# A two-layer selective-scan block: softplus from one Exp, carries and products two states at a time, old y added on VectorE

## The chip, the cores and the metric

One core of a Trainium2 chip runs the whole program. The metric is device time in microseconds (us) of one execution, the median of three runs. The engines are named as the profile names them: PE (TensorE, with PEld for its weight loads), DVE (VectorE), ACT (ScalarE), POOL (GpSimd) and SP, whose queue issues the DMAs.

## What is computed

Two layers of a vision state-space model work on x of shape (4, 64, 64, 192) in fp32. Only the first layer is touched. For each of 4 images it makes u (384 channels at 4096 positions) and a gate z by a projection, and then runs four selective scans: k = 0 along rows, k = 1 along columns, k = 2 and 3 the same two backwards. Cut to what matters:

```python
delta = jax.nn.softplus(delta + delta_bias[None, :, None])
def step(h, inp):
    dt, ut, bt, ct = inp
    dA = jnp.exp(dt[..., None] * A_k[None])
    dBu = dt[..., None] * bt[:, :, None, :] * ut[..., None]
    h = dA * h + dBu
    y = jnp.einsum('bkdn,bkn->bkd', h, ct)
    return (h, y)
# 16 states n, 384 channels d, 4096 steps, 4 directions k, 4 images
y = out_y[:, 0] + inv_y[:, 0] + wh_y + invwh_y     # the four directions are summed
```

A normalisation, the gate and an output projection follow. The second layer is of the same kind, written in another way.

## The kernel before

The method `scans` of `FirstLayer` runs once per image. An **item** is one direction k and one chunk of 512 positions: 4 x 8 = 32 items per image, first those of k = 0 and 2 alternating, then, from item 16, those of k = 1 and 3. Each item goes through 16 **states** n, so a step of the main loop is one state of one item, numbered g; an image has 512 of them. A tile of 128 partitions x 3 x 512 holds the 384 channels as three blocks d of 128.

One state of one item takes:

- ACT: `b_product` (L716), four scalings of dt*u by B, token by token, two states ahead; `decay` (L728), three Exps with a scale per partition, one state ahead.
- PE: `turn_x` (L733), three times four transposes of 128 x 128 that bring the product from tokens to channels in PSUM; the tile x has three buffers.
- DVE: `scan` (L741), three scans of 512 columns that read a from SBUF and x from PSUM and write h. After the third, a small tensor_reduce (L751) copies the last column of the three blocks into a tile `carry`, from which the next item of this direction starts.
- POOL: `c_product` (L755), h times C over 128 x 1536, in place. It can't begin before the reduce has read h.
- PE: `add_y` (L768), three times four transposes that add h into the item's y in PSUM (tiles yp), three states later. Because yp has one buffer, states 0 and 1 of an item are added in its state 4, and state 2, 3, ... in its state 5, 6, ...

The tile h has seven buffers of one state each. y of the four directions is summed in DRAM: `load("yold")` fetches what is there, `start_y` (L762) puts it into yp by a matmul with the identity in states 3 and 4, `end_y` (L781) copies yp out on DVE in states 2 and 3 of the next item, and a DMA stores it. yold is fetched in state 5 for the item after it, if that has the same kind of direction; otherwise, at item 16, only when the item before has been stored, in state 3.

All four engines run in an order written out by hand, and each engine takes its instructions in that order. In step g the order is: ACT's prepared steps, b_product(g+2), decay(g+1); then for each block d: scan(g, d) on DVE, turn_x(g+1, d) on PE, and the add_y steps that are due on PE; then PE's prepared steps, c_product(g) and POOL's prepared steps. The prepared steps make delta, B and dt*u of coming items. The method `steps` of `Item` lists each as (items ahead, state, engine, function); those of (2, 13) run in state 13 of the item two before. Softplus is computed as max(v, 0) + log(1 + e), with e = exp(-|v|):

- `dt_rows` (L632): v from a matmul of 13 rows into PSUM, in states 7 to 9 two items ahead and once more in states 5 to 7 one item ahead. The PSUM tiles dp, tp, bp and zp share two buffers.
- `absolute` (L638) and `exp` (L641) on ACT in states 10 to 12 and 13, into tile e, which has one buffer.
- `plus` (L645) and `minus` (L649) on POOL in states 14 and 15: 1 + e rounded, and what remains when 1 is taken away again; `log` (L652) on ACT, `rest` (L655) and `total` (L658) on POOL in states 2, 1 and 4 one item ahead. `rest` and `total` add what the rounding lost, so that small delta stay exact.
- `delta` (L661) on DVE in states 7 to 9, then `turn` (L675) and `times_u` (L681) in states 10 to 13.

The first eight items of an image also make the gate: one matmul step on PE and one copy on ACT in each of three states (`gate_in`, `gate_out`).

Of the kernel before, what the change touches and what calls it, by code (L numbers as in the profile page):

```python
# [10 lines left out]
F32 = mybir.dt.float32  # L11
# [8 lines left out]
LC = 512  # L20
# [382 lines left out]
class FirstLayer:  # L403
# [168 lines left out]
    def scans(self):  # L572
        nc, tc = self.tc.nc, self.tc
        with ExitStack() as ctx:
            pool = lambda name, bufs, **k: ctx.enter_context(tc.tile_pool(name=name, bufs=bufs, **k))
            p1, p2, p3, p7 = pool("b1", 1), pool("b2", 2), pool("b3", 3), pool("b7", 7)
# [4 lines left out]
            ident = self.ident  # L581
# [22 lines left out]
            class Item:  # L604
# [30 lines left out]
                def absolute(self, d):  # L635
                    if d == 0:
                        self.e = p1.tile([128, ND, LC], F32, name="e")
                    nc.scalar.activation(self.e[:, d, :], self.dp[d], AF.Abs)  # L638

                def exp(self):  # L640
                    nc.scalar.activation(self.e, self.e, AF.Exp, scale=-1.0)  # L641

                def plus(self):
                    self.wl = p1.tile([128, ND, LC], F32, name="wl")
                    nc.gpsimd.tensor_scalar(self.wl, self.e, 1.0, 1.0, ALU.add, ALU.mult)  # L645

                def minus(self):
                    self.dt = p2.tile([128, ND, LC], F32, name="dt")
                    nc.gpsimd.tensor_scalar(self.dt, self.wl, -1.0, 1.0, ALU.add, ALU.mult)  # L649

                def log(self):
                    nc.scalar.activation(self.wl, self.wl, AF.Ln)  # L652

                def rest(self):
                    nc.gpsimd.tensor_tensor(self.e, self.e, self.dt, ALU.subtract)  # L655

                def total(self):
                    nc.gpsimd.tensor_tensor(self.e, self.e, self.wl, ALU.add)  # L658

                def delta(self, d):  # L660
                    nc.vector.scalar_tensor_tensor(  # L661
                        self.dt[:, d, :], self.dp[d], 0.0, self.e[:, d, :], ALU.max, ALU.add
# [22 lines left out]
                def steps(self):  # L685
# [3 lines left out]
                    for d in range(ND):  # L689
                        r += [(2, 7 + d, "pe", s(self.dt_rows, d)), (2, 10 + d, "act", s(self.absolute, d))]  # L690
                    r += [(2, 13, "act", self.exp), (2, 14, "pool", self.plus), (2, 14, "pool", self.load_u)]
                    r += [(2, 15, "pool", self.minus), (1, 2, "act", self.log)]
# [17 lines left out]
            carry, xTs, xs, as_, hs, cs = {}, {}, {}, {}, {}, {}  # L710
# [26 lines left out]
            def scan(g, d):  # L737
                it, n = flat[g]
                if d == 0:
                    hs[g] = p7.tile([128, ND, LC], F32, name="h")  # L740
# [4 lines left out]
                    0.0 if it.first else carry[it.k, n][:, d : d + 1],  # L745
# [3 lines left out]
                if d == ND - 1:  # L749
                    kept = carry[it.k, n] = pk.tile([128, ND], F32, name=f"carry{it.k // 2}_{n}")  # L750
                    nc.vector.tensor_reduce(kept, last(hs[g], it.k), mybir.AxisListType.X, ALU.max)  # L751
# [5 lines left out]
            def start_y(it, b):  # L757

                if b == 0:
                    it.yp = [ps_y.tile([128, LC], F32, name=f"yp{i}") for i in range(ND)]  # L760
                yo = it.yold.rearrange("p j e -> p (j e)")[:, b * LC : (b + 1) * LC]
                nc.tensor.matmul(it.yp[b], ident, yo, start=True, stop=False, skip_group_check=True)  # L762

            def add_y(g, b):
                it, n = flat[g]
                for i in range(NJ):
# [5 lines left out]
                        start=False,  # L772
# [5 lines left out]
            def end_y(it, b):  # L778
                if b == 0:
                    it.yt = p1.tile([128, NJ, DI], F32, name="yt")  # L780
                nc.vector.tensor_copy(it.yt.rearrange("p j e -> p (j e)")[:, b * LC : (b + 1) * LC], it.yp[b])  # L781
# [16 lines left out]
            with tc.manual_schedule(engines={nc.tensor.engine, nc.scalar.engine, nc.vector.engine, nc.gpsimd.engine}):  # L798
# [18 lines left out]
                items[0].yold = load("yold", self.y_dram, items[0].k, items[0].c)  # L817
# [8 lines left out]
                for g in range(N + LAG + 1):  # L826
# [11 lines left out]
                    if it is not None:  # L838
                        for at, b in (((LAG, 1), 0), ((LAG, 2), 1), ((LAG + 1, 0), 2)):
# [793 lines left out]
```

## Time and profile before

| what | us |
|---|---|
| median of 3 runs | 11103.35 (11099.11 to 11105.88) |
| the profiled execution's own time | 11106.54 |
| its span, first to last instruction | 11104.6 |
| DVE busy | 9693.3 (87%) |
| ACT busy | 9775.8 (88%) |
| POOL busy | 8587.9 (77%) |
| PE busy | 9551.9 (86%) |
| one scan stage, first to last c_product of an image | 2192 to 2197, four times |

Some of the costliest groups of instructions of the first layer's scans (duration: mean of one):

| line, engine | what | count | ns |
|---|---|---|---|
| L755 POOL | h times C | 2048 | 3470 |
| L741 DVE | scan with a carry | 5376 | 1266 |
| L716 ACT | b_product | 8192 | 609 |
| L728 ACT | decay | 6144 | 716 |
| L751 DVE | carry | 2048 | 158 |
| L762 PE | old y into PSUM | 768 | 664 |
| L638, L641, L652 ACT | Abs; Exp; Log | 384; 128; 128 | 585; 1478; 1485 |
| L645, L649 POOL | plus; minus | 128; 128 | 1478; 1482 |
| L655, L658 POOL | rest; total | 128; 128 | 3460; 3477 |

Instructions of one engine overlap, so the distance from one start to the next is shorter than a duration. A wait is shown as idle time with the engine and line that ended it. PE's clock is granted at full or half rate, and the trace has a record of it.

### The profile page before, as it was taken

The numbers are of one execution on the slowest core, as the hardware profiler recorded it, in microseconds if no ns is written. First come the engines' busy times: TensorE is split into PE (matmuls) and PEld (weight loads), VectorE is DVE, ScalarE is ACT, GpSimd is POOL, SyncE is SP. The second block draws the span as 40 slices with busy tenths as digits, with TensorE's granted clock in tenths as the row PEclk, the third lists the DMA queues.
The fourth block names the chain that finished last, engine by engine and source line by source line (L and its number), as shares of the span: only waits on it lengthen the run. The fifth ranks groups of instructions, "written<-read, shape, count | busy, mean of one in ns | idle before, by whom it ended". The sixth has DMA issues, their size and how long they took to land. (4 is left out here: it accounts for less than half of the span.)

```text
span 11104.6 us, 172135 instructions
## 1 busy us (share of the span) xinstructions
PE 9551.9 (86%) x61449; PEld 7273.6 (66%) x61449; DVE 9693.3 (87%) x11515; ACT 9775.8 (88%) x16979; POOL 8587.9 (77%) x2776
## 2 busy tenths in 40 slices
PE   7998888888988888888988888889988888788677
PEld 4776666666776666656776666657766766655366
DVE  4999899976999899968999899949998999878675
ACT  5999999977999999969999999959999999856477
POOL 3999899955999899938999899929998999700370
PEclk8999999998999999998999999989999999989688
DMA  4333344344333344443333433353333434433458
GB/s 125 109 108 101 91 101 101 98 137 127 109 106 101 92 101 99 98 159 112 109 103 96 98 97 99 93 168 109 109 99 95 98 98 98 120 119 123 157 131 272
DMA packets 833671, 1267.54 MB, mean 114 GB/s; under 512 B 102026, under 2 KB 517655, under 8 KB 832292
## 3 DMA queue, kind: packets, MB, share of 16 engines
q1 hardware_dynamic: 827940, 1250.15, 40.5%
q0 software_dynamic: 4864, 6.29, 0.4%
q8 instruction: 488, 8.00, 0.3%
q14 instruction: 379, 3.10, 0.1%
HBM read 955.83 MB, written 300.42 MB: 113 GB/s over the span
## 5 line engine op out<-in xcount | busy, mean ns | idle before, releaser
L755 POOL TENSOR_TENSOR h<-h,bct 128x1536 f32<-128x1536 f32 x2048 | 7062.9, 3470 | 579.9 <-DVE carry L751 477.5
L741 DVE TENSOR_TENSOR_SCAN h<-a,carry,x 128x512 f32<-128x512 f32 x5376 | 6604.9, 1266 | 231.0 <-PE x L733 194.9
L733 PE MATMUL x<-ident,xT 128*128 128x128 f32 x24576 | 4000.8, 287 | 811.8 <-DVE h L741 710.1
L716 ACT ACTIVATE xT<-dtuT,bT 128x384 f32<-128x384 f32 x8192 | 4358.8, 609 | 93.0 <-PE x L733 87.3
L733 PEld LDWEIGHTS x<-ident,xT 128*128 128x128 f32 x24576 | 2804.0, 145 | 2136.5 <-DVE h L741 920.5
L728 ACT ACTIVATE a<-dt,A_log_f 128x512 f32<-128x512 f32 x6144 | 3977.7, 716 | 0.0
L768 PE MATMUL yp<-ident,h 128*128 128x128 f32 x24576 | 3703.1, 277 | 9.2 <-POOL h L755 9.2
L768 PEld LDWEIGHTS yp<-ident,h 128*128 128x128 f32 x24576 | 2944.2, 144 | 78.8 <-issue 62.6
L632 PE MATMUL dp<-xd,w_dtb_f 13*128 13x512 f32 x1536 | 882.7, 657 | 216.0 <-DVE dt L661 211.3
L741 DVE TENSOR_TENSOR_SCAN h<-a,x 128x512 f32<-128x512 f32 x768 | 899.1, 1207 | 191.3 <-PE x L733 114.0
L645 POOL TENSOR_SCALAR wl<-e 128x1536 f32<-128x1536 f32 x128 | 189.2, 1478 | 799.3 <-ACT e L641 406.2
L519 PE MATMUL pp<-xT,w_in 96*128 96x512 f32 x1152 | 539.2, 617 | 1.1 <-DVE xw L562 1.1
L632 PEld LDWEIGHTS dp<-xd,w_dtb_f 13*128 13x128 f32 x1536 | 235.0, 189 | 456.6 <-DVE dt L661 341.3
L762 PE MATMUL yp<-yold,ident 128*128 128x512 f32 x768 | 445.1, 664 | 72.7 <-DMA yold<-y 72.7
L1137 DVE SCALAR_TENSOR_TENSOR acc<-pad,conv_w_s,acc 128x2048 f32<-128x2048 f32 x192 | 439.3, 2342 | 53.5 <-ACT acc L1135 52.9
L638 ACT ACTIVATE e<-dp 128x512 f32<-128x512 f32 x384 | 224.7, 585 | 269.3 <-DVE dt L661 155.4
L1118 POOL MEMSET pad<- 128x66 f32 x12 | 1.9, 158 | 578.4 <-DVE acc L1137 458.9
L658 POOL TENSOR_TENSOR e<-e,wl 128x1536 f32<-128x1536 f32 x128 | 445.1, 3477 | 0.3
L655 POOL TENSOR_TENSOR e<-e,dt 128x1536 f32<-128x1536 f32 x128 | 442.9, 3460 | 0.3
L751 DVE TENSOR_REDUCE carry<-h 128x3 f32<-128x3 f32 x2048 | 322.7, 158 | 70.4
L519 PEld LDWEIGHTS pp<-xT,w_in 96*128 96x128 f32 x1152 | 221.3, 198 | 244.4 <-issue 234.3
L661 DVE SCALAR_TENSOR_TENSOR dt<-dp,e 128x512 f32<-128x512 f32 x384 | 255.5, 666 | 65.2 <-POOL e L658 58.7
(170 smaller groups left out, 6875.3 us busy)
## 6 DMA issues: line engine op xcount, KB each, us to landing
bct<-xp SPq DMA_DIRECT2D x1024, 512.0 KB, 4.9
uT<-uT SPq DMA_DIRECT2D x64, 768.0 KB, 4.7
yold<-y SPq DMA_DIRECT2D x64, 768.0 KB, 7.9
y<-yt SPq DMA_DIRECT2D x64, 768.0 KB, 4.5
uT<-uT SPq DMA_DIRECT2D x128, 384.0 KB, 5.0
yold<-y SPq DMA_DIRECT2D x128, 384.0 KB, 5.3
y<-yt SPq DMA_DIRECT2D x128, 384.0 KB, 4.6
zg<-gate SPq DMA_DIRECT2D x64, 768.0 KB, 6.3
```

The costliest lines, as they stand in the source:

```text
L519: self.tc.nc.tensor.matmul(pp, self.w_in[:, i, e * 128 : (e + 1) * 128], self.xT[:, i, t * LC : (t + 1) * LC], start=(i == 0), stop=(i == ...
L632: nc.tensor.matmul(self.dp[d], w, self.xd[0 : DR + 1, :], start=True, stop=True)
L655: nc.gpsimd.tensor_tensor(self.e, self.e, self.dt, ALU.subtract)
L658: nc.gpsimd.tensor_tensor(self.e, self.e, self.wl, ALU.add)
L716: nc.scalar.mul(xTs[g][:, j, :], it.dtuT[:, j * DI : (j + 1) * DI], it.bT[:, j, n : n + 1])
L728: nc.scalar.activation(as_[g][:, d, :], it.dt[:, d, :], AF.Exp, scale=scale)
L733: nc.tensor.transpose(xs[g, d][:, j * 128 : (j + 1) * 128], xTs[g][:, j, d * 128 : (d + 1) * 128], ident)
L741: nc.vector.tensor_tensor_scan(along(hs[g][:, d, :], it.k), along(as_[g][:, d, :], it.k), along(xs.pop((g, d)), it.k), 0.0 if it.first els ...
L755: nc.gpsimd.tensor_tensor(hs[g], hs[g], bc(cs[g - n % 2][:, n % 2, :], 1, ND), ALU.mult)
L762: nc.tensor.matmul(it.yp[b], ident, yo, start=True, stop=False, skip_group_check=True)
L768: nc.tensor.matmul(it.yp[b][:, i * 128 : (i + 1) * 128], hs[g][:, d, j * 128 : (j + 1) * 128], ident, start=False, stop=n == NS - 1, is_tr ...
L1137: nc.vector.scalar_tensor_tensor(acc, part(tap), weight(tap), acc, ALU.mult, ALU.add)
```

## The change

Three things are done in `scans`.

**Softplus.** ACT takes e = exp(v) straight from PSUM, one block at a time in states 10 to 12. POOL makes m = min(e, 1) (`cap`, state 13) and dt = (m + 1) - 1 (`rounded`, state 15); ACT takes log(e + 1) with a bias tile of ones, `rest` is m - dt, `total` adds it, and `delta` is max(min(e, 30), v) with v still in PSUM. The instructions on POOL and DVE keep their number and shape; ACT has one of 1536 columns less.

**Pairs of states.** h becomes a tile of two states, with three buffers. The last columns of an even and the following odd state are copied by one tensor_reduce after the odd one (128 x 6 elements), and both c_products come after it, in the odd step, ahead of POOL's prepared steps of that step.

**Old y.** `start_y` and its matmuls go; the first transposes of state 0 open the accumulation in yp. `end_y` adds yold to yp on DVE where it copied before. yold is fetched in state 8 of its own item, for every item.

```diff
-                def absolute(self, d):
+                def exp(self, d):
                     if d == 0:
                         self.e = p1.tile([128, ND, LC], F32, name="e")
-                    nc.scalar.activation(self.e[:, d, :], self.dp[d], AF.Abs)
-                def exp(self):
-                    nc.scalar.activation(self.e, self.e, AF.Exp, scale=-1.0)
-                def plus(self):
-                    self.wl = p1.tile([128, ND, LC], F32, name="wl")
-                    nc.gpsimd.tensor_scalar(self.wl, self.e, 1.0, 1.0, ALU.add, ALU.mult)
-                def minus(self):
+                    nc.scalar.activation(self.e[:, d, :], self.dp[d], AF.Exp)
+                def cap(self):
+                    self.m = p1.tile([128, ND, LC], F32, name="m")
+                    nc.gpsimd.tensor_scalar(self.m, self.e, 1.0, 1.0, ALU.min, ALU.mult)
+                def rounded(self):
                     self.dt = p2.tile([128, ND, LC], F32, name="dt")
-                    nc.gpsimd.tensor_scalar(self.dt, self.wl, -1.0, 1.0, ALU.add, ALU.mult)
+                    nc.gpsimd.tensor_scalar(self.dt, self.m, 1.0, -1.0, ALU.add, ALU.add)
                 def log(self):
-                    nc.scalar.activation(self.wl, self.wl, AF.Ln)
+                    nc.scalar.activation(self.e, self.e, AF.Ln, bias=one)
                 def rest(self):
-                    nc.gpsimd.tensor_tensor(self.e, self.e, self.dt, ALU.subtract)
+                    nc.gpsimd.tensor_tensor(self.m, self.m, self.dt, ALU.subtract)
                 def total(self):
-                    nc.gpsimd.tensor_tensor(self.e, self.e, self.wl, ALU.add)
+                    nc.gpsimd.tensor_tensor(self.e, self.e, self.m, ALU.add)
                 def delta(self, d):
                     nc.vector.scalar_tensor_tensor(
-                        self.dt[:, d, :], self.dp[d], 0.0, self.e[:, d, :], ALU.max, ALU.add
+                        self.dt[:, d, :], self.e[:, d, :], 30.0, self.dp[d], ALU.min, ALU.max
                     )
...
-                        r += [(2, 7 + d, "pe", s(self.dt_rows, d)), (2, 10 + d, "act", s(self.absolute, d))]
-                    r += [(2, 13, "act", self.exp), (2, 14, "pool", self.plus), (2, 14, "pool", self.load_u)]
-                    r += [(2, 15, "pool", self.minus), (1, 2, "act", self.log)]
+                        r += [(2, 7 + d, "pe", s(self.dt_rows, d)), (2, 10 + d, "act", s(self.exp, d))]
+                    r += [(2, 13, "pool", self.cap), (2, 14, "pool", self.load_u)]
+                    r += [(2, 15, "pool", self.rounded), (1, 2, "act", self.log)]
...
-                if d == 0:
-                    hs[g] = p7.tile([128, ND, LC], F32, name="h")
+                if d == 0 and n % 2 == 0:
+                    both[g] = p3.tile([128, 2, ND, LC], F32, name="h")
+                    hs[g], hs[g + 1] = both[g][:, 0], both[g][:, 1]
...
-                if d == ND - 1:
-                    kept = carry[it.k, n] = pk.tile([128, ND], F32, name=f"carry{it.k // 2}_{n}")
-                    nc.vector.tensor_reduce(kept, last(hs[g], it.k), mybir.AxisListType.X, ALU.max)
+                if d == ND - 1 and n % 2:
+                    kept = carry[it.k, n - 1] = pk.tile([128, 2, ND], F32, name=f"carry{it.k // 2}_{n}")
+                    nc.vector.tensor_reduce(kept, last(both.pop(g - 1), it.k), mybir.AxisListType.X, ALU.max)
...
-                nc.tensor.matmul(it.yp[b], ident, yo, start=True, stop=False, skip_group_check=True)
...
-                        start=False,
+                        start=n == 0 and i == 0,
...
-                nc.vector.tensor_copy(it.yt.rearrange("p j e -> p (j e)")[:, b * LC : (b + 1) * LC], it.yp[b])
+                part = slice(b * LC, (b + 1) * LC)
+                yt, yo = (t.rearrange("p j e -> p (j e)")[:, part] for t in (it.yt, it.yold))
+                nc.vector.tensor_add(yt, it.yp[b], yo)
...
                         prepare(g, "pe")
-                        c_product(g)
+                        if n % 2:
+                            c_product(g - 1)
+                            c_product(g)
                         late.append(g)
                         prepare(g, "pool")
-                        if n == 5 and i + 1 < len(items) and items[i + 1].k % 2 == it.k % 2:
-                            q = items[i + 1]
-                            q.yold = load("yold", self.y_dram, q.k, q.c)
+                        if n == 8:
+                            it.yold = load("yold", self.y_dram, it.k, it.c)
```

More of the change, by code (lines that the diff above doesn't have):

```diff
@@ L575, in scans @@
             pool = lambda name, bufs, **k: ctx.enter_context(tc.tile_pool(name=name, bufs=bufs, **k))
-            p1, p2, p3, p7 = pool("b1", 1), pool("b2", 2), pool("b3", 3), pool("b7", 7)
+            p1, p2, p3 = pool("b1", 1), pool("b2", 2), pool("b3", 3)
             pk = pool("ca", 2)
@@ L580, in scans @@
             ps_m = pool("psm", 2, space=bass.MemoryType.PSUM)
-            ident = self.ident
+            ident, one = self.ident, self.one
             n8 = LC // HW
@@ L709, in scans @@
             N = len(flat)
-            carry, xTs, xs, as_, hs, cs = {}, {}, {}, {}, {}, {}
+            carry, xTs, xs, as_, hs, cs, both = {}, {}, {}, {}, {}, {}, {}
             def b_product(g):
@@ L744, in scan @@
                     along(xs.pop((g, d)), it.k),
-                    0.0 if it.first else carry[it.k, n][:, d : d + 1],
+                    0.0 if it.first else carry[it.k, n - n % 2][:, n % 2, d : d + 1],
                     ALU.mult,
@@ L755, in c_product @@
                 nc.gpsimd.tensor_tensor(hs[g], hs[g], bc(cs[g - n % 2][:, n % 2, :], 1, ND), ALU.mult)
[L757 to L762, printed above, removed]
             def add_y(g, b):
                 it, n = flat[g]
+                if n == 0 and b == 0:
+                    it.yp = [ps_y.tile([128, LC], F32, name=f"yp{i}") for i in range(ND)]
                 for i in range(NJ):
@@ L815, in prepare @@
                             f()
-                items[0].yold = load("yold", self.y_dram, items[0].k, items[0].c)
                 c_rows(0)
@@ L837, in scans @@
                     adds = [[] for _ in range(ND)]
-                    if it is not None:
-                        for at, b in (((LAG, 1), 0), ((LAG, 2), 1), ((LAG + 1, 0), 2)):
-                            if at[0] == n:
-                                adds[at[1]].append((start_y, it, b))
                     ready = [x for x in late if x <= g - LAG and (n > LAG or x // NS < i)][:2]
@@ L853, in scans @@
                             end_y(before, {2: 0, 0: 1, 1: 2}[d])
-                            if (n, d) == (LAG, 1) and it is not None and it.yold is None:
-                                it.yold = load("yold", self.y_dram, it.k, it.c)
                         if g + 1 < N:
```

## The prediction

> **What bounds the kernel now.** I read the waits first, then busy time over one item, then the timelines of VectorE (DVE), ScalarE (ACT), GpSimd (POOL) and TensorE (PE) over that item. The waits:
>
> ```profile
> engine line waited for: us in total, times, longest us
> PEld dp L632 <- DVE dt L661: 341.3, 223, 12.1
> PE dp L632 <- DVE dt L661: 211.3, 204, 10.5
> ACT e L638 <- DVE dt L661: 155.4, 108, 2.6
> PE yp L762 <- DMA yold<-y: 72.7, 4, 18.4
> ```
>
> The last is four stops of 18 us, one per image, where direction k changes. The others are a ring: delta on DVE (L661) lets PE's dt rows (L632) into a PSUM buffer and lets ACT into tile e (L638). One item, 1500 to 1568.5:
>
> ```profile
> core 0: us, PE busy (x) PEld busy (x) DVE busy (x) ACT busy (x) POOL busy (x), PEclk, DMA share, GB/s
> 1500.00:1568.50 68.50, 60.57 (x424) 47.41 (x423) 66.32 (x76) 67.37 (x121) 65.58 (x21) 0.98 0.38 102
> ```
>
> Three engines lie within 2 us of each other, so each must be followed. VectorE:
>
> ```profile
> 1499.33 3.62 DVE L741 TENSOR_TENSOR_SCAN h<-a,carry,x 128x512 f32<-128x512 f32 x3
> 1502.99 0.16 DVE L751 TENSOR_REDUCE carry<-h 128x3 f32<-128x3 f32 x1
> 1503.10 3.62 DVE L741 TENSOR_TENSOR_SCAN h<-a,carry,x 128x512 f32<-128x512 f32 x3
> ...
> 1541.85 0.67 DVE L661 SCALAR_TENSOR_TENSOR dt<-dp,e 128x512 f32<-128x512 f32 x1
> 1542.43 1.27 DVE L741 TENSOR_TENSOR_SCAN h<-a,carry,x 128x512 f32<-128x512 f32 x1
> 1543.74 0.16 DVE L751 TENSOR_REDUCE carry<-h 128x3 f32<-128x3 f32 x1
> 1544.38 2.45 DVE L741 TENSOR_TENSOR_SCAN h<-a,carry,x 128x512 f32<-128x512 f32 x2 [0.49 <-PE x L733]
> ```
>
> A plain state takes 3.77 us (1503.10 - 1499.33) without a gap: VectorE sets the pace. Averaging the start of each state's first scan over the items after the eighth, away from the change of direction, states 0 to 15 take 3.77, 3.89, 4.38, 4.95, 3.77, 3.89, 3.77, 4.34, 4.89, 5.14, 4.48, 4.56, 4.37, 4.36, 3.77, 3.76: together 68.1 us. Only states 8 to 10 hold true waits, for x from PE, which sits behind dt rows that wait for delta. The eight items per image that also make the gate take 69.4. ScalarE is the one that waits:
>
> ```profile
> 1547.53 0.60 ACT L638 ACTIVATE e<-dp 128x512 f32<-128x512 f32 x1 [1.13 <-DVE dt L661]
> ...
> 1560.58 1.47 ACT L641 ACTIVATE e<-e 128x1536 f32<-128x1536 f32 x1
> ```
>
> GpSimd has slack only late in the item; from state 14 to state 10 it works off a queue:
>
> ```profile
> 1523.36 10.36 POOL L755 TENSOR_TENSOR h<-h,bct 128x1536 f32<-128x1536 f32 x3
> 1533.64 3.49 POOL L658 TENSOR_TENSOR e<-e,wl 128x1536 f32<-128x1536 f32 x1
> 1537.07 20.58 POOL L755 TENSOR_TENSOR h<-h,bct 128x1536 f32<-128x1536 f32 x6
> 1558.44 3.48 POOL L755 TENSOR_TENSOR h<-h,bct 128x1536 f32<-128x1536 f32 x1 [0.80 <-DVE carry L751]
> ```
>
> Here total (L658) runs behind the product of state 4. A product takes (20.58 - 3.48)/5 = 3.42 start to start, a tensor_scalar 1.44 (1506.79 to 1508.22).
>
> **What the Trainium skill says.** "ScalarE: Activation LUTs", What ACT_TABLE_LOAD costs: every function costs the same per element, 186 ns + 0.833 N, and a per-partition pointer operand adds some 93 ns. The trace agrees: 0.585 us for 512 columns, 1.48 for 1536. "VectorE: DVE Perf Modes", The perf-mode tier table: fp32 work with a PSUM operand runs at one element per cycle whether it copies or adds; the trace has 674 ns for the copy (L781) and 674 for a product of PSUM and SBUF (L681). "GPSIMD Engine Reference", Specifications: GpSimd shares its SBUF interface with VectorE, which disturbs it where an instruction has two SBUF inputs. The new add has one, so I charge nothing; the products stay within 3.41 to 3.57 us before. "TensorE: Matmul & The Clock Gate", Part 1: the clock goes to half after an idle window of 3.41 us, free-running. The trace's clock record agrees and sharpens it: in the scan stages it holds 130 dips, 93 in states 8 to 10 and 34 in state 3, nearly all one window long. Counting dt-row matmuls (13 of 128 rows) at a tenth, a window with fewer than 11 transposes (1.2 us at 0.11 each) was followed by half clock 88 times in 89; one with over 14, practically never.
>
> **The change, part by part.**
>
> *Softplus.* Abs and Exp become one Exp: ScalarE loses 1.38 us per item (1560.58 to the next start at 1561.96); Log's bias tile adds 0.09. ScalarE's own work falls from 66.0 to 64.7 us (67.7 to 66.4 with the gate). It wasn't the pace: gain nothing in plain items; what is late next is delta, for which it already waited. GpSimd keeps four steps at the same prices (min against add isn't in the trace: 1.44, between 1.4 and 1.6), but cap comes at state 13 where plus came at 14. At each image's start the chain is serial and loses 1.5 us for item 0 and 1.4 for item 1: -12 us in four images.
>
> *Carries in pairs.* A reduce costs 3.77 - 3 x 1.175 = 0.245 us with the drain ahead of it; eight per item go. Six elements instead of three: nothing measurable, at most 0.02. In states 8 and 10 the pace is PE's, so 6 x 0.245 = 1.5 us are worth having, if nothing else ends the wait.
>
> *Products in pairs.* Both now follow the odd state. GpSimd's queue is the same work in another order: products 12, 13, cap, 14, 15, rounded, 0, 1, rest, 2, 3, **total, then 4**. Take the start of state 14 as zero. Product 12 starts at 0.25, and from there nothing lets GpSimd idle: nine products, 2 x 1.44 and two more tensor_tensors: 0.25 + 30.8 + 2.9 + 6.8 = 40.75 us for the end of product 4. (The same count on the old order gives 34.3, 6.15 after state 4's last scan; the trace has 6.23.) PE reaches add_y of state 4 in its step 7, just behind the transposes for the first scan of state 8. Those need the PSUM buffer that the first scan of state 7 frees at 36.0 (34.75 + 1.2), and PE, busy without a gap from state 5 to 7, is some 1.4 us late for it: it stops at 37.9. Queued behind it are the transposes for the second scan of state 8: 0.44 for the adds, 0.66 for them, 0.15 for two semaphores: that scan starts at 42.0. Without the stop VectorE would be there at 40.26 (the states above, less 0.245 in 14, 0, 2, 4 and 6, plus 1.18); before, it was there at 41.5. So the whole gain of the reduces up to there is gone, and 0.5 us more. Three pairs of h instead of seven tiles: pair (4,5) is free at some 48, wanted at 50.6; no wait. Last product of an image: 3.42 later, four times, +14 us.
>
> *Old y on VectorE.* Three fp32 matmul steps of 1.02 us leave PE per item; the adds cost what the copies cost. PE isn't the pace there. But state 3 now leaves PE only 12 transposes between 19.2 and 25.0, so a window under 11 comes in every item; the dip falls on state 4's adds, costs PE about 1 us and is covered, because PE would stop at 37.9 anyway. The stop itself (2 to 2.9 us idle, with dt rows and four transposes before it) makes such a window for about 85% of phases. That dip lies on the path: adds, transposes and dt rows at half rate put state 9 at 46.9 instead of 45.8. In return the dips after the dt rows should mostly go: PE is now late for them, the 1.0 us gap between them closes, and 2.1 us of dt rows alone don't make a poor window. State 9 then takes 4.9 and state 10 3.75, as in items without a dip today.
>
> *yold's load* moves to state 8 of its own item, needed one item later; on SP's queue it passes row loads wanted some 20 us later. The four stops go. The items there take 86.4, 85.0, 84.9 and 85.1 us.
>
> **Sum.** New item: 46.9 + 4.9 + 3.75 + 4.56 + 4.12 + 4.36 = 68.6 us. Plain items 92 x (+0.5) = +46; gate items 32 x (68.6 - 69.4) = -26; four changes of direction 4 x (68.6 - 85.35) = -67; start and end +2. Total -45 on the profiled execution's 11106.5 (span 11104.6); that run lies 3 over the median, so about 11060.
>
> **The rivals.** A change under 0.2% (22 us) is no change that a measurement of this kernel can tell.
> - *No stop* (12%): GpSimd's late products don't reach VectorE, all 1.5 us of reduces count, gate items lose 2: -135 - 64 - 75 + 2, 10830. For: products had 3.6 us of slack or more on average. Against: the 6.4 us by which product 4 moves.
> - *Stop without a dip on the path* (15%): state 9 at 45.8, item 67.5: -55 - 61 - 71 + 2, 10918.
> - *Forecast* (50%): 11020 to 11110.
> - *Two dips, slower* (20%): the dip at the stop comes and the old ones in states 8 to 10 stay, 0.95 us per item (0.25 in 9, 0.7 in 10, against items without): 69.55, +133 + 5 - 63 + 2, 11180. Over today's time once 0.35 us of it stays, so if the old dips survive in some 37% of items.
> - *The pair isn't split* (3%): add_y of state 4 waits for the pair's second product too, 3.4 us per item, 11495. Against: a first scan starts up to 1.2 us ahead of its state's last decay, so parts of a tile are kept apart.
>
> Range 10880 to 11215. It leaves out the first and last and the edges of the others. Faster 0.61 (the first two and two thirds of the forecast), same 0.18, slower 0.21.
>
> **What would show it.** PE waiting at yp for POOL some 2 to 3 us per item, 25 us in total before, 250 to 400 after; VectorE waiting for x at state 8's second scan; dips in states 3/4 and 7/8 and few in 9; no yold wait; ACT idle of 2 us or more per item. No PE wait for POOL means the first rival; the old dips at 9 mean the fourth.

## The result, and the profile after

| | us |
|---|---|
| before, median of 4 runs | 11101.23 (11093.25 to 11105.88) |
| after, median of 4 runs | 12045.64 (12032.84 to 12063.36) |
| ratio | 1.0855 (95%: 1.0842 to 1.0868) |
| predicted | 11060, range 10880 to 11215 |

The change makes the kernel 8.5% slower, and the prediction was wrong, in sign and far outside its range. The profiled executions took 11106.54 and 12063.36, a difference of 957. The four scan stages, first scan to last, make 8788 before and 9715 after, so 927 of it lie there; the serial start of an image, from the first Abs or Exp to the first scan, grew from 35.2 to 40.5 on average, another 21 for four images. That leaves 9 us for everything else.

The costliest groups of after that the change touches (count, busy time, mean ns of one, idle time before them and what ended most of it):

```profile
L754 POOL TENSOR_TENSOR h<-h,bct 128x1536 f32<-128x1536 f32 x2048 | 7035.1, 3463 | 577.7 <-DVE carry L750 537.7
...
L643 POOL TENSOR_SCALAR m<-e 128x1536 f32<-128x1536 f32 x128 | 689.8, 5389 | 801.5 <-ACT e L639 801.5
...
L647 POOL TENSOR_SCALAR dt<-m 128x1536 f32<-128x1536 f32 x128 | 690.8, 5397 | 0.7
L639 ACT ACTIVATE e<-dp 128x512 f32<-128x512 f32 x384 | 224.9, 586 | 393.4 <-DVE dt L659 271.8
...
L777 DVE TENSOR_TENSOR yt<-yp,yold 128x512 f32<-128x512 f32 x384 | 258.9, 675 | 68.2 <-PE yp L762 67.3
```

Two lines stand out. `cap` (L643) and `rounded` (L647) take 5389 and 5397 ns, where `plus` and `minus` took 1478 and 1482 on tiles of the same shape. Before they read:

```profile
L649 POOL TENSOR_SCALAR dt<-wl 128x1536 f32<-128x1536 f32 x128 | 189.6, 1482 | 0.7
L645 POOL TENSOR_SCALAR wl<-e 128x1536 f32<-128x1536 f32 x128 | 189.2, 1478 | 799.3 <-ACT e L641 406.2 <-DMA xp<-xw 393.1
```

Everything else costs what it did: the products 3463 against 3470, Exp from PSUM 586 against 585 for Abs, the add of old y 675 against 674 for the copy. Two steps that are 3.9 us longer, 128 times, are 1002 us more work for GpSimd.

The waits of after:

```profile
engine line waited for: us in total, times, longest us
DVE h L740 <- PE x L731: 1241.9, 1150, 5.1
PEld yp L762 <- POOL h L754: 1004.4, 425, 4.7
ACT xT L714 <- PE x L731: 985.8, 539, 5.4
PE yp L762 <- POOL h L754: 896.6, 376, 4.4
...
POOL h L754 <- DVE carry L750: 537.7, 305, 3.7
ACT e L639 <- DVE dt L659: 271.8, 116, 3.5
```

The stop at yold is gone, as it should be. In place of the ring through delta stands another: PE waits 897 us in `add_y` for GpSimd's products, VectorE waits 1242 for x from PE (309 before), and GpSimd waits 538 for the reduce on VectorE (478 before). PE's wait was next to nothing before:

```profile
PE yp L768 <- POOL h L755: 9.2, 8, 2.2
```

One item of after, 1701 to 1778:

```profile
core 0: us, PE busy (x) PEld busy (x) DVE busy (x) ACT busy (x) POOL busy (x), PEclk, DMA share, GB/s
1701.00:1778.00 77.00, 62.18 (x415) 51.89 (x414) 64.86 (x67) 66.09 (x118) 72.24 (x20) 0.89 0.34 88
```

An item now lasts 77.0 us, and GpSimd is busy for 72.2 of it; VectorE and ScalarE do a little less than before and are idle for 12 and 11. GpSimd's timeline over the same item (start us, us, what, count, in brackets idle time before it and what ended it):

```profile
1701.02 6.89 POOL L754 TENSOR_TENSOR h<-h,bct 128x1536 f32<-128x1536 f32 x2 [1.58 <-DVE carry L750]
1707.87 5.39 POOL L643 TENSOR_SCALAR m<-e 128x1536 f32<-128x1536 f32 x1
1713.23 6.86 POOL L754 TENSOR_TENSOR h<-h,bct 128x1536 f32<-128x1536 f32 x2
1720.05 5.40 POOL L647 TENSOR_SCALAR dt<-m 128x1536 f32<-128x1536 f32 x1
1725.42 6.86 POOL L754 TENSOR_TENSOR h<-h,bct 128x1536 f32<-128x1536 f32 x2
1732.23 3.47 POOL L653 TENSOR_TENSOR m<-m,dt 128x1536 f32<-128x1536 f32 x1
1735.66 6.83 POOL L754 TENSOR_TENSOR h<-h,bct 128x1536 f32<-128x1536 f32 x2
1742.43 3.46 POOL L656 TENSOR_TENSOR e<-e,m 128x1536 f32<-128x1536 f32 x1
1745.85 20.53 POOL L754 TENSOR_TENSOR h<-h,bct 128x1536 f32<-128x1536 f32 x6
1769.55 6.89 POOL L754 TENSOR_TENSOR h<-h,bct 128x1536 f32<-128x1536 f32 x2 [3.18 <-DVE carry L750]
1778.03 3.46 POOL L754 TENSOR_TENSOR h<-h,bct 128x1536 f32<-128x1536 f32 x1 [1.59 <-DVE carry L750]
```

The order is the one counted in the prediction: 12, 13, cap, 14, 15, rounded, 0, 1, rest, 2, 3, total, 4. Product 4 ends at 1745.85 + 3.42 = 1749.27, 48.25 us after product 12 began. The prediction had 40.5 from there; with 5.37 start to start (1713.23 - 1707.87 and 1725.42 - 1720.05, rounded) instead of 1.44 for the two steps its count gives 48.4. So the counting was sound, and one number in it was not. What GpSimd is late for is seen on PE, in its timeline over the same item:

```profile
1716.73 1.11 PE L762 MATMUL yp<-ident,h 128*128 128x128 f32 x4 [3.01 <-POOL h L754]
1717.64 1.06 PE L731 MATMUL x<-ident,xT 128*128 128x128 f32 x4
...
1734.85 0.60 PE L731 MATMUL x<-ident,xT 128*128 128x128 f32 x4
1739.15 1.12 PE L762 MATMUL yp<-ident,h 128*128 128x128 f32 x4 [3.70 <-POOL h L754]
1740.05 1.06 PE L731 MATMUL x<-ident,xT 128*128 128x128 f32 x4
```

The timeline of VectorE shows who waits behind PE:

```profile
1735.66 1.28 DVE L740 TENSOR_TENSOR_SCAN h<-a,carry,x 128x512 f32<-128x512 f32 x1
1741.22 1.28 DVE L740 TENSOR_TENSOR_SCAN h<-a,carry,x 128x512 f32<-128x512 f32 x1 [4.28 <-PE x L731]
1742.86 1.28 DVE L740 TENSOR_TENSOR_SCAN h<-a,carry,x 128x512 f32<-128x512 f32 x1 [0.35 <-PE x L731]
```

PE stops twice in an item: at the adds of state 14 (its product starts behind cap and ends at 1716.65) and at those of state 2 (behind rest, 1739.08). Each time four transposes for VectorE's next scan stand behind the adds in PE's order, so the second scans of states 2 and 6 come 2.1 and 3.9 us late, on average over the items. Behind both stops shown, four transposes take 1.06 us instead of 0.60: PE runs at half clock, which its record has from 1715.24 and from 1739.13. The record has 368 dips (stretches at half clock) in the scan stages, where before had 130. By state 10 GpSimd has caught up and waits for the reduce of each pair (3.18 and 1.59 above); those 4.8 us are what an item has beyond GpSimd's work.

State by state, from the start of one first scan to the next, averaged as in the prediction (items after the eighth, without items 15 to 17 at the change of direction, counted from 0, and the last; `log_apart` is an experiment below):

```
state       0    1    2    3    4    5    6    7    8    9    10   11   12   13   14   15   sum
before     3.77 3.89 4.38 4.95 3.77 3.89 3.77 4.34 4.89 5.14 4.48 4.56 4.37 4.36 3.77 3.76  68.1
after      3.54 3.87 6.98 4.95 3.54 4.75 9.55 4.99 5.19 5.09 4.23 4.55 4.14 4.34 3.54 3.74  77.0
log_apart  3.54 3.87 4.12 4.96 3.54 4.66 3.70 4.34 6.18 5.04 4.23 4.56 4.14 4.34 3.54 3.74  68.5
```

The reduces did go where they should: states 0, 4 and 14 are 0.23 us shorter. They are worth 1.8 us in an item, and states 2 and 6 alone cost 8.4.

### The profile page after: what moved, and what is told of

Its sections match the earlier page's. It is cut to its first block, busy times and chain, and to the rows that moved or that the text cites. A ratio compares the mean times of both kernels' runs of the same rounds, so it can differ in the third digit from the quotient of the medians.

```text
span 12061.6 us, 168561 instructions
## 1 busy us (share of the span) xinstructions
PE 9800.1 (81%) x60681; PEld 7738.8 (64%) x60681; DVE 9580.0 (79%) x10491; ACT 9666.5 (80%) x16851; POOL 9561.0 (79%) x2776
## 5 line engine op out<-in xcount | busy, mean ns | idle before, releaser
L754 POOL TENSOR_TENSOR h<-h,bct 128x1536 f32<-128x1536 f32 x2048 | 7035.1, 3463 | 577.7 <-DVE carry L750 537.7
L731 PE MATMUL x<-ident,xT 128*128 128x128 f32 x24576 | 4247.2, 300 | 754.0 <-DVE h L740 683.6
L762 PE MATMUL yp<-ident,h 128*128 128x128 f32 x24576 | 4105.2, 298 | 899.0 <-POOL h L754 896.6
L731 PEld LDWEIGHTS x<-ident,xT 128*128 128x128 f32 x24576 | 3068.7, 153 | 1820.0 <-issue 774.8
L762 PEld LDWEIGHTS yp<-ident,h 128*128 128x128 f32 x24576 | 3246.1, 156 | 1009.6 <-POOL h L754 1004.4
L643 POOL TENSOR_SCALAR m<-e 128x1536 f32<-128x1536 f32 x128 | 689.8, 5389 | 801.5 <-ACT e L639 801.5
L647 POOL TENSOR_SCALAR dt<-m 128x1536 f32<-128x1536 f32 x128 | 690.8, 5397 | 0.7
L653 POOL TENSOR_TENSOR m<-m,dt 128x1536 f32<-128x1536 f32 x128 | 443.7, 3466 | 0.3
L656 POOL TENSOR_TENSOR e<-e,m 128x1536 f32<-128x1536 f32 x128 | 443.5, 3465 | 0.3
L659 DVE SCALAR_TENSOR_TENSOR dt<-e,dp 128x512 f32<-128x512 f32 x384 | 254.6, 664 | 80.8 <-POOL e L656 74.3
L777 DVE TENSOR_TENSOR yt<-yp,yold 128x512 f32<-128x512 f32 x384 | 258.9, 675 | 68.2 <-PE yp L762 67.3
```

The lines of the kernel that those rows point to most:

```text
L643: nc.gpsimd.tensor_scalar(self.m, self.e, 1.0, 1.0, ALU.min, ALU.mult)
L647: nc.gpsimd.tensor_scalar(self.dt, self.m, 1.0, -1.0, ALU.add, ALU.add)
L653: nc.gpsimd.tensor_tensor(self.m, self.m, self.dt, ALU.subtract)
L656: nc.gpsimd.tensor_tensor(self.e, self.e, self.m, ALU.add)
L731: nc.tensor.transpose(xs[g, d][:, j * 128 : (j + 1) * 128], xTs[g][:, j, d * 128 : (d + 1) * 128], ident)
L754: nc.gpsimd.tensor_tensor(hs[g], hs[g], bc(cs[g - n % 2][:, n % 2, :], 1, ND), ALU.mult)
```

## The experiments

The theory after this reading: the price of the two GpSimd steps is the cause, and PE's adds pass it on. The rivals: that the order of the paired products is the cause, whatever the steps cost; that the new flow of softplus is (what Log or delta wait for); that the old y on VectorE is, by the clock. All times below are medians, each beside before's on the same chip.

| kernel | us | before | ratio (95%) |
|---|---|---|---|
| fast_steps | 11093.76 | 11103.14 | 0.9989 (0.9981 to 0.9997) |
| before_add_add | 11943.75 | 11103.14 | 1.0756 (1.0739 to 1.0772) |
| old_y_alone | 11074.28 | 11103.14 | 0.9970 (0.9958 to 0.9982) |
| op_prices | 11409.65 (one run) | 11103.14 | |
| free_log | 12344.11 | 11103.54 | 1.1115 (1.1099 to 1.1130) |
| pairs_alone | 11377.83 | 11103.54 | 1.0240 (1.0226 to 1.0254) |
| softplus_alone | 11953.75 | 11103.54 | 1.0764 (1.0748 to 1.0781) |
| exp_old_y | 11036.72 | 11103.54 | 0.9936 (0.9923 to 0.9950) |
| log_apart | 11031.80 | 11104.46 | 0.9930 (0.9916 to 0.9943) |
| log_apart_lag4 | 11067.77 | 11104.46 | 0.9964 (0.9950 to 0.9977) |
| old_y_warm | 11029.56 | 11102.94 | 0.9934 (0.9921 to 0.9948) |
| log_apart_warm | 11049.64 | 11102.94 | 0.9959 (0.9946 to 0.9973) |

### fast_steps: the changed kernel with the old pair of operations

```diff
-                    nc.gpsimd.tensor_scalar(self.m, self.e, 1.0, 1.0, ALU.min, ALU.mult)
+                    nc.gpsimd.tensor_scalar(self.m, self.e, 1.0, 1.0, ALU.add, ALU.mult)
...
-                    nc.gpsimd.tensor_scalar(self.dt, self.m, 1.0, -1.0, ALU.add, ALU.add)
+                    nc.gpsimd.tensor_scalar(self.dt, self.m, -1.0, 1.0, ALU.add, ALU.mult)
...
-                    nc.scalar.activation(self.e, self.e, AF.Ln, bias=one)
+                    nc.scalar.activation(self.m, self.m, AF.Ln)
...
-                    nc.gpsimd.tensor_tensor(self.m, self.m, self.dt, ALU.subtract)
+                    nc.gpsimd.tensor_tensor(self.e, self.e, self.dt, ALU.subtract)
```

> The changed kernel with GpSimd's two tensor_scalar steps in the form of the kernel before (add then multiply, 1.44 us each by the trace of before) at the places where cap and rounded stand; everything else as changed: one Exp from PSUM, pairs of states, old y on VectorE. Theory 1, the price of the two steps: they took 5.39 and 5.40 us in the changed kernel where the prediction had 1.44, 7.9 us per item on GpSimd. Then this kernel is what the prediction costed: about 11060 us, between 10900 and 11200, item 68.6 us, the late scan is the second of state 8. Theory 2, the pairs: putting both products after the odd state is what costs; then the time stays over 11700 us with the steps at 1.44.

Measured 11094, 952 less than after, with pairs, Exp from PSUM and old y on VectorE all in place. That leaves nothing of the 8.5% to them. The time lies between the 10900 and 11200 expected, but not for the reason expected: state 8 (4.86 us) doesn't show the forecast's stop. State 2 is long instead (6.43), for a reason that this edit brought in itself: Log now takes the rounded sum m, and has to wait until `rounded` has read it, behind products 14 and 15. ScalarE's timeline:

```profile
1639.66 1.49 ACT L650 ACTIVATE m<-m 128x1536 f32<-128x1536 f32 x1 [3.09 <-POOL dt L647]
```

VectorE's timeline a few us later:

```profile
1643.81 1.28 DVE L740 TENSOR_TENSOR_SCAN h<-a,carry,x 128x512 f32<-128x512 f32 x1 [2.19 <-ACT a L726]
```

Decay and b_product stand behind Log on ScalarE; the scan waits for decay. The forecast's own step is therefore not yet tested.

### before_add_add: the kernel before with the new pair

```diff
-                    nc.gpsimd.tensor_scalar(self.wl, self.e, 1.0, 1.0, ALU.add, ALU.mult)
+                    nc.gpsimd.tensor_scalar(self.wl, self.e, 1.0, 0.0, ALU.add, ALU.add)
...
-                    nc.gpsimd.tensor_scalar(self.dt, self.wl, -1.0, 1.0, ALU.add, ALU.mult)
+                    nc.gpsimd.tensor_scalar(self.dt, self.wl, -1.0, 0.0, ALU.add, ALU.add)
```

> The kernel before, with its two GpSimd steps written as add then add of zero instead of add then multiply by one; the same values, nothing else changed. Theory 1: the steps take 5.4 us, GpSimd's work per item goes from 64.5 to 72.4 us, over the 68.1 us of today's item, and with the 2 to 4 us that GpSimd idles per item the item takes 73 to 76 us: 11700 to 12100 us in all. Theory 2: the steps' price is no matter without the pairs; under 11350 us.

Measured 11944: another operation in two instructions costs the untouched kernel 841 us. The way it takes is another than in after. A line of this kernel's waits has Log waiting for `minus`:

```profile
ACT wl L652 <- POOL dt L649: 831.4, 124, 11.0
```

That is 6.7 us each time, and state 2 grows from 4.38 to 10.72. So the price is the cause in both kernels, and who is held up by it depends on what stands behind the late step.

### op_prices: the step in eight forms

`plus` is done with one of eight pairs, one per item in turn; the softplus of those items is another function than the reference's.

```diff
+            PAIRS = [(1.0, ALU.add, 1.0, ALU.mult), (1.0, ALU.mult, 1.0, ALU.add), (-1.0, ALU.subtract, 1.0, ALU.mult),
+                     (1.0, ALU.add, 0.0, ALU.subtract), (1.0, ALU.add, 0.0, ALU.max), (0.0, ALU.max, 1.0, ALU.add),
+                     (1.0, ALU.add, None, None), (2.0, ALU.min, 1.0, ALU.add)]
...
-                    nc.gpsimd.tensor_scalar(self.wl, self.e, 1.0, 1.0, ALU.add, ALU.mult)
+                    a, op0, b, op1 = PAIRS[items.index(self) % 8]
+                    nc.gpsimd.tensor_scalar(self.wl, self.e, a, b, op0, *([op1] if op1 else []))
```

> The kernel before, where the first GpSimd step of each item makes the same e + 1 with one of eight pairs of operations by the item's number: add and multiply, multiply and add, subtract and multiply, add and subtract, add and max, max and add, add alone, min and add. Theory 1: two prices only, 1.44 us and 5.4 us, and the pairs of an add with a multiply are the cheap ones; the single add I can't tell. Rival: the price hangs on min alone or on the constants, and add with subtract or max costs 1.44 us.

Five items in a row, from GpSimd's timeline (start us, us):

```profile
1033.34 5.39 POOL L646 TENSOR_SCALAR wl<-e 128x1536 f32<-128x1536 f32 x1
...
1104.52 4.10 POOL L646 TENSOR_SCALAR wl<-e 128x1536 f32<-128x1536 f32 x1
...
1175.83 5.39 POOL L646 TENSOR_SCALAR wl<-e 128x1536 f32<-128x1536 f32 x1
...
1248.15 1.48 POOL L646 TENSOR_SCALAR wl<-e 128x1536 f32<-128x1536 f32 x1
...
1315.19 1.48 POOL L646 TENSOR_SCALAR wl<-e 128x1536 f32<-128x1536 f32 x1
```

These are max with add, a lone add, min with add, add with mult, mult with add. The means of 16 of each, with those of after:

```
add, mult       1.478 us      add, max        5.385 us
mult, add       1.480         max, add        5.389
add alone       4.099         min, add        5.395
add, subtract   5.397         min, mult       5.389  (after, L643)
subtract, mult  5.394         add, add        5.397  (after, L647)
```

In the eight forms of this run, shape, type and buffers are one and the same, so the operations set the time. Only a multiplication and an addition together, in either order, take 1.48 (with a factor of 1, the only one tried); each other pair tried takes 5.4, and an addition alone is dearer than with a multiplication by 1 behind it. Two prices were expected, with the lone addition left open; it has a third.

### old_y_alone: the third part by itself

```diff
-                nc.tensor.matmul(it.yp[b], ident, yo, start=True, stop=False, skip_group_check=True)
...
-                        start=False,
+                        start=n == 0 and i == 0,
...
-                nc.vector.tensor_copy(it.yt.rearrange("p j e -> p (j e)")[:, b * LC : (b + 1) * LC], it.yp[b])
+                nc.vector.tensor_add(yt, it.yp[b], yo)
```

> The kernel before with the third part alone: old y added on VectorE where it is copied out, its load in state 8 of its own item, no matmuls for it. Theory 1 (the prediction's steps): the four stops of 17 us at the change of direction go, the rest of the item is unchanged, 11035 us; TensorE's clock dips in state 3 of every item but without cost. Rival: the emptier state 3 costs TensorE's clock on the path, 1 us per item, and the result is 11160 us or no change.

Measured 11074, 29 less than before. Item 16 takes 65.8 us instead of 85.2, four times: -78. The rest is given back: plain items take 68.7 instead of 68.1, and the clock's record has 217 dips, of which 124 lie in states 3 and 4 (37 before): in state 3 PE now has nothing but 12 transposes to do. States 5 and 10 grow by 0.3 and 0.2 us. The expectation had these dips at no cost, 11035 in all; its rival had them at 1 us an item.

### softplus_alone and pairs_alone

The first is the kernel before with the softplus of after as it stands; the second with pairs only:

```diff
-                    hs[g] = p7.tile([128, ND, LC], F32, name="h")
+                    both[g] = p3.tile([128, 2, ND, LC], F32, name="h")
...
-                        c_product(g)
+                        if n % 2:
+                            c_product(g - 1)
+                            c_product(g)
```

> The kernel before with the first part alone, softplus as the change writes it (min then multiply, add then add; Log from e). Theory 1: both GpSimd steps take 5.4 us, GpSimd has 72.4 us per item and idles little, the item takes 73 to 75 us and the whole 11700 to 12000 us: nearly all of the loss. Theory 2 (the price hurts only together with the pairs): under 11500 us.

> The kernel before with the second part alone: carries and products in pairs of states, softplus and old y as before. Theory 1: like fast_steps, since Log waits for minus behind the pair 14, 15: the reduces' 1.5 to 2 us are given back in state 2; item 68.7, stops at the change of direction kept: 11150 us, 11100 to 11200. Theory 2 (the pairs are the costly part): over 11350 us.

Softplus alone gives 11954, +850. Its PE waits 396 us in `add_y` for the products, and the second scan of state 6 comes 3.7 us late: the same stop as in after, with products that aren't paired. Pairs alone give 11378, +274, where 11150 was expected: a miss, and within the "over 11350" of its second theory, that the pairs are the costly part. In fast_steps, with the same pairs, the whole takes 11094; what makes the pairs dearer beside the rest of the kernel before is shown only in part. Products 14 and 15 now go ahead of `minus`, and Log waits for `minus`, up to 3.5 us, as a line of the waits of pairs_alone has it:

```profile
ACT wl L652 <- POOL dt L649: 278.2, 110, 3.5
```

State 2 takes 6.43 us as in fast_steps (4.38 before), and states 5 and 10 grow by 1.0 and 0.6. The clock's record has 113 dips in state 3 and 60 in state 10 (34 and 4 before), which fits, but no run shows that they are the cause. The three parts alone make 850 + 274 - 29 = +1095, together +944: they don't add. One difference is that in after Log takes e and need not wait for the rounding.

### free_log: a miss of my own

This was to be fast_steps with Log freed from the rounding. The edit missed its aim: Log takes e in state 2, but `rest` has written the remainder over e in state 1, so the log is that of the remainder and the softplus is not the reference's. Against fast_steps, Log changes so (and `total` adds the new tile):

```diff
-                    nc.scalar.activation(self.m, self.m, AF.Ln)
+                    self.l = p1.tile([128, ND, LC], F32, name="l")
+                    nc.scalar.activation(self.l, self.e, AF.Ln, bias=one)
```

> fast_steps with ScalarE's Log taken from e with a bias of one into a tile of its own, so that it waits for no GpSimd step. In fast_steps VectorE stood 2.3 us in state 2 of every item, for a decay behind Log, which waited for the step that stands where rounded does. Theory 1 (the prediction's chain of products): with Log free the stop in state 2 goes, the product of state 4 ends some 13.5 us after its last scan instead of 11.2, and the stop appears where it was predicted, at the second scan of state 8: item again 68 to 69 us, 11040 to 11110 us in all. Rival (no stop at state 8: the products' queue is absorbed): item 66.4, 10830 to 10900 us.

Measured 12344. In its waits Log stands still for `rest`, which comes behind products 14 to 1 and `rounded` in GpSimd's queue:

```profile
ACT l L651 <- POOL e L654: 1568.8, 124, 13.9
```

It tells nothing of the theory. It does show the price of a Log that waits: 12.7 us an item on average in this line, and state 2 grows to 16.67.

### log_apart: the forecast's own case

Cheap steps, and the data flow of after: Log from e into a tile of its own, the remainder into m.

```diff
-                    nc.gpsimd.tensor_scalar(self.m, self.e, 1.0, 1.0, ALU.min, ALU.mult)
+                    nc.gpsimd.tensor_scalar(self.m, self.e, 1.0, 1.0, ALU.add, ALU.mult)
...
-                    nc.gpsimd.tensor_scalar(self.dt, self.m, 1.0, -1.0, ALU.add, ALU.add)
+                    nc.gpsimd.tensor_scalar(self.dt, self.m, -1.0, 1.0, ALU.add, ALU.mult)
...
-                    nc.scalar.activation(self.e, self.e, AF.Ln, bias=one)
+                    self.l = p1.tile([128, ND, LC], F32, name="l")
+                    nc.scalar.activation(self.l, self.e, AF.Ln, bias=one)
...
-                    nc.gpsimd.tensor_tensor(self.m, self.m, self.dt, ALU.subtract)
+                    nc.gpsimd.tensor_tensor(self.m, self.e, self.dt, ALU.subtract)
...
-                    nc.gpsimd.tensor_tensor(self.e, self.e, self.m, ALU.add)
+                    nc.gpsimd.tensor_tensor(self.e, self.l, self.m, ALU.add)
```

> What free_log was meant to be: the changed kernel with both GpSimd steps as add then multiply, Log from e with a bias of one into a tile of its own, and rest written beside e, so that Log waits for no GpSimd step, as in the changed kernel. (free_log's Log came behind rest, which had overwritten e: it took the log of the remainder and waited some 14 us per item.) Theory 1, the prediction's chain of products: no stop in state 2; product 4 ends some 13.5 us after its last scan; VectorE stops 1.5 to 3 us at the second scan of state 8; item 68 to 69.5 us, 11020 to 11110 us in all. Rival, the queue is absorbed: item 66.4, 10830 to 10900 us.

Measured 11032, ratio 0.993. Its steps take the old prices, as its groups show:

```profile
L647 POOL TENSOR_SCALAR dt<-m 128x1536 f32<-128x1536 f32 x128 | 189.9, 1484 | 0.7
L643 POOL TENSOR_SCALAR m<-e 128x1536 f32<-128x1536 f32 x128 | 189.4, 1479 | 777.5 <-ACT e L639 777.5
```

And here is the stop that the prediction worked out, at the adds of state 4, here in one item, in PE's timeline:

```profile
1649.35 0.66 PE L732 MATMUL x<-ident,xT 128*128 128x128 f32 x4
1651.58 0.66 PE L763 MATMUL yp<-ident,h 128*128 128x128 f32 x4 [1.57 <-POOL h L755]
1652.07 0.60 PE L732 MATMUL x<-ident,xT 128*128 128x128 f32 x4
```

And VectorE's, with the second scan of state 8:

```profile
1650.63 1.28 DVE L741 TENSOR_TENSOR_SCAN h<-a,carry,x 128x512 f32<-128x512 f32 x1
1652.78 1.28 DVE L741 TENSOR_TENSOR_SCAN h<-a,carry,x 128x512 f32<-128x512 f32 x1 [0.87 <-PE x L732]
```

PE waits 181 us for products in all, 1.4 per item. Against after only the two pairs of operations (so m is e + 1, not min(e, 1)) and the tiles in which the results lie differ, and the time is 1014 us less.

### exp_old_y: without pairs

Old y on VectorE and Exp from PSUM, with `plus`, `minus` and single products as before:

```diff
-                    nc.scalar.activation(self.e[:, d, :], self.dp[d], AF.Abs)
+                    nc.scalar.activation(self.e[:, d, :], self.dp[d], AF.Exp)
...
-                        self.dt[:, d, :], self.dp[d], 0.0, self.e[:, d, :], ALU.max, ALU.add
+                        self.dt[:, d, :], self.e[:, d, :], 30.0, self.dp[d], ALU.min, ALU.max
```

> The kernel before with old y added on VectorE and with one Exp from PSUM, but GpSimd's steps left as add then multiply and products state by state. Expected: ScalarE's 1.4 us per item matter only in items that make the gate: 11074 of old_y_alone less 32 times 0.5 to 1 us, 11040 to 11065 us. Rival: ScalarE was on the path after all and 128 times 1.4 us come off: 10900 us.

Measured 11037, 3 under the range expected. Its interval and that of log_apart lie over each other: beside the other two parts, pairs bring nothing that this measurement can tell.

### log_apart_lag4 and the warm kernels: can more be had?

log_apart_lag4 adds h to yp four states later instead of three, so that no product is late. To make room for a fourth pair of h, the new y is made in yold's tile, the tile of B and C (bct) has two buffers instead of three, and the projection's weight is loaded once per image:

```diff
-                    both[g] = p3.tile([128, 2, ND, LC], F32, name="h")
+                    both[g] = p4.tile([128, 2, ND, LC], F32, name="h")
...
-                LAG = 3
+                LAG = 4
```

> log_apart with one more pair of h (four) and the adds of y four states behind instead of three; to make room y is added in yold's own tile, the rows of C have two buffers and a projection weight is loaded per image. If TensorE's stop for a late product is what keeps the reduces' gain from showing, it goes: no wait of TensorE for products, item 66 to 67 us, 10800 to 10920 us. If the queue on GpSimd itself is the bound, the item stays at 68 us or more and the time at that of log_apart.

The warm kernels put three matmuls without use where `start_y` stood, in states 3 and 4, in old_y_alone and in log_apart. The first add of the item overwrites what they leave:

```diff
+            def keep_warm(it, b):
+                nc.tensor.matmul(it.yp[b], ident[0:CB, :], self.xT[:, 0, 0:LC], start=True, stop=False, skip_group_check=True)
```

> old_y_alone with three matmuls of no use at the places in states 3 and 4 where the old y was put into PSUM before (96 rows of the projection's input, overwritten by the first add of y); no load waits for them. old_y_alone has 124 of its 217 clock dips in states 3 and 4 (before: 37 of 130) and an item of 68.7 us. If the emptier TensorE is what costs 0.6 us per item there, the dips fall to some 130, the item to 68.1 us and the time from 11074 to 11000 to 11030 us. If the dips cost nothing, 11074 or more.

> log_apart with the same three matmuls. By the chain of products the second scan of state 8 comes 42 us after the start of state 14 whatever VectorE does before it, since product 4 is what it waits for: the dips in states 3 and 4 go and state 5 gets some 0.6 us shorter, state 8 as much longer; item 68.3 to 68.6, 11010 to 11040 us, no gain beyond 0.2%. If the dips are the bound there, the item falls to 67.8 us and the time under 10980 us.

lag4 gave 11068: a miss. PE hardly waits for products any more (16 us in all), and the stop in state 8 is gone, yet plain items take 68.1 and gate items (2 to 6 of an image) 71.4, against 68.5 and 69.35 in log_apart. State 6 takes 5.41 now (3.70 in log_apart). PE has 24 adds in its state 5, 124 of 212 dips lie in states 4 and 5, and VectorE's first scan of state 7 comes 1.1 us late. So taking away the stop let another one out; that the adds and the clock make it is argued, not shown. Why the gate items lose 2 us was not followed up; the edits made for room may have a part in it.

old_y_warm gave 11030, as expected: dips fall from 217 to 128, plain items from 68.7 to 68.2. So most of what old_y_alone lost in plain items was the clock's. log_apart_warm gave 11050, above the 11010 to 11040 expected: dips fall from 180 to 117 and nothing is won. State 5 gets 0.24 us shorter and state 8 0.64 longer, which fits that there the product of state 4 holds PE up, not the clock; 70 of the 93 dips in state 3 stay. By the ratios it is even 0.3% slower than log_apart, and why stays open. log_apart, exp_old_y and old_y_warm all beat before by 0.6 to 0.7%, and their intervals don't tell them apart.

## Why the prediction was wrong, point by point

**The step that failed** is in the part on softplus: "GpSimd keeps four steps at the same prices (min against add isn't in the trace: 1.44, between 1.4 and 1.6)". They take 5.37 start to start. Two things were wrong with it. Every tensor_scalar on GpSimd in the trace of before was add with mult; neither min with mult nor add with add was there, and the second was priced as if it had been. And the bounds of 1.4 and 1.6 came from no row. The next row of the same engine, shape and type was the tensor_tensor's 3.42, and with that the sum would have rung: 16 x 3.42 + 2 x 3.42 + 6.8 = 68.4 us of GpSimd in an item counted at 68.6. The whole forecast stood on the steps staying under some 3.5 us, and no rival had them above it. Of the two on the slower side, one was about the clock and one about the split of the pair. The Trainium skill, "GPSIMD Engine Reference", Engine selection, calls one-input work on GpSimd roughly line-rate, and two-input work slower. That reads like one price for all one-input steps; the runs show three, 1.48, 4.10 and 5.39 us, and the last two are above the 3.46 of a two-input product.

**GpSimd's queue.** Right, with its order and its arithmetic: 48.4 with the measured price against 48.25 in after. With the cheap steps, product 4 was to end 40.75 us after the start of state 14; in log_apart it ends at 40.86.

**The stop at state 4's adds.** Right in log_apart: VectorE's second scan of state 8 was to start 42.0 us after state 14; it starts at 42.15. In after the same mechanism acts two states earlier and once more at state 14, because 3.9 us more stand ahead of the product of state 14 and 7.9 ahead of that of state 2. PE's wait at yp for POOL was to be 2 to 3 us per item: it is 1.4 in log_apart (181 us in all) and 7.0 in after (897). The 25 us that the prediction gave for before are the waits of PE and of its weight loads together (9.2 + 16.2); counted so, log_apart has 393, within the 250 to 400 forecast.

**The clock.** Half right. State 3 does leave PE too little (93 dips there in log_apart, 34 before), and of the 93 dips in states 8 to 10 before, 55 are left, 35 of them in 9: fewer, but not few. The dip in states 3 and 4 comes in nearly every item, as said (124 for 128 items). But the dip at the stop itself, put at 85% of items, hardly comes: 17 in state 8. The stop was to last 2 to 2.9 us and lasts 1.4, which may be why. State 9 therefore starts at 46.2, not 46.9, and states 9 and 10 take 5.04 and 4.23, not 4.9 and 3.75. These errors cancel: 68.5 us an item against 68.6 predicted. That the sum fits is thus in part luck.

**Softplus on ScalarE.** Right: Exp from PSUM costs what Abs did, Log with a bias tile took 1572 ns, +0.087 (0.09 predicted), and an image's serial start is 2.7 us shorter in log_apart (2.9 predicted). In after the dear steps make it 5.3 longer.

**Carries.** Right: a reduce of six elements takes 163 ns, of three 158, and 0.23 us per pair goes. Up to state 8 the stop swallows them, as said.

**Old y.** Right in sign and place: no stop at yold, item 16 at 67.1 in log_apart (68.6 predicted), state 3 without enough work for the clock. Part of it is given back in item 17, which takes 71.5 on average (68.3 before), with 10.1 in state 8: in the second image PE waits 2.40 us there for the product of state 4. As a part alone old y is worth -29 us, not the -67 of its stops.

**The total.** With 1.44 put right by the experiment instead of in the sum, the forecast's case measures 11032 (11060 predicted). The mechanisms held; the one price that wasn't measured decided the sign.

## What to carry to other kernels

A price read from a trace is the price of the operations that the trace has, not of every instruction of that name, shape and type: where the pair of operations is new, bound it by every other row of that engine and ask at which price the engine becomes the pace. Count a queue in its new order, and look for the in-order engine that waits for its late end and for what stands behind that wait; the same late step held up PE in one kernel here and ScalarE in another. Parts measured alone don't add: here their sum missed the whole by 150 us.

## What the runs showed of the hardware that was not expected

- A tensor_scalar of 128 x 1536 fp32 on GpSimd takes 1.48 us as add with mult or mult with add, 5.38 to 5.40 in seven other pairs, and 4.10 as an addition alone. To leave an operation out made the instruction 2.8 times as long.
- Three matmuls without use per item made old_y_alone faster by 45 us (11074 to 11030, each beside its own before), with PE's clock kept up: 217 dips became 128.
- Half clock came with the longer stops of PE: in the item shown of after, behind waits of 3.0 and 3.7 us, four transposes took 1.06 us instead of 0.60; behind one of 1.57 in the item shown of log_apart they took 0.60. Over the whole run, the clock's record has half rate within 3 us after 179 of the 206 stops of 3 us or more ahead of adds in after, and after 15 of the 96 stops of 1 to 2 us in log_apart.
